# Four transposes of the identity behind every transpose of a gathered block, in the first stage of a recommender kernel

## The chip, the cores and the metric

The kernel runs on one core of a Trainium2 chip. The metric is the time of one execution on the device, in microseconds (us); smaller is better. Times of a kernel are medians of several runs. Engines are named as in the profile: PE is TensorE's matmul, PEld its weight load, DVE is VectorE, ACT is ScalarE, POOL is GpSimd and SP is SyncE. L335 is line 335 of the kernel before.

## What is computed

There are B = 1024 users with T = 50 items each, and a table of N = 100001 item embeddings of D = 128 numbers. For each user the running mean of the gathered embeddings is taken, normalised over the users, and sent through a spiking neuron; the spikes are averaged over time, and the averages are multiplied with the whole table.

```python
emb = emb_table.at[0].set(0.0)
e = emb[seq]                                   # 1024 x 50 x 128
prefix = jnp.cumsum(e, axis=1)
denom = jnp.minimum(t_idx[None, :], lengths[:, None]).astype(e.dtype)
uF = prefix / denom[:, :, None]
mean, var = uF.mean(axis=0), uF.var(axis=0)
y = (uF - mean) * lax.rsqrt(var + BN_EPS) * gamma + beta

def step(v, x):
    v = v + (x - v) / TAU
    spike = atan_spike(v - V_TH)
    return (v - spike * V_TH, spike)
_, spikes = lax.scan(step, v0, jnp.moveaxis(y, 1, 0))
scores = spikes.mean(axis=0) @ emb.T           # 1024 x 100001
```

## The kernel before

The kernel has two stages. The order of the work on every engine is written out by hand (`manual_schedule`): each engine runs its instructions in program order, and waits only where one needs what another engine has made.

**First stage: 50 steps, one for each position t.** Embeddings lie transposed on the chip, D on the 128 partitions and the 1024 users along the free axis, in two halves h of 512.

- `gather(t)` (L207) issues eight indirect DMAs from POOL, each fetching 128 rows of the table into a block of the tile `e`. There are two tiles `e`, used in turn; gather(t + 2) is issued in step t and overwrites the tile that step t reads, so it waits until TensorE has read it.
- For each of the eight blocks TensorE transposes the block by a matmul with the identity (L324) and adds it to the running sum `pre[h]` in PSUM. Half 0 has the first four blocks, half 1 the last four.
- After each half DVE makes the running mean `uF` from `pre[h]` (L335) and its statistics (L336).
- `correct(t + 1)` (L282) then adds to each half of `pre` a matmul that cancels row 0 of the table. It overwrites what L335 has read, so each of the two waits for the L335 of its half, and the next step's transposes come after both.
- DVE and ACT turn the statistics into scale and shift and update the membrane `v`, the reset and the count of spikes (L298, L301, L353, L376, L379, L294). This is one chain from step to step.
- In steps 42 and 44 the first two blocks of the table are prepared for the second stage: eight plain transposes each (L136) and a split into two parts by ACT (L152) and DVE (L153).

`keep_busy(tile, times)` (L308 to L310) issues transposes of a tile into `warm`, a PSUM tile of two banks that nothing reads and that becomes the tile `po0` of the second stage afterwards. In the kernel before it is called in the last step only: four transposes of the identity behind each of the first three blocks of half 1 (L333, L334), and sixteen of `near` after the loop (L415).

**Second stage.** The counts (1024 x 128) are multiplied with the table, block by block: transposes of a table block (L136), a split into two parts, products into PSUM (L160), a scaled copy by DVE or ACT (L512, L514), and stores of the 410 MB of scores by SP. Its first products wait for the count of the first 128 users (`countA`, L367), the end of the first stage's chain.

Of the kernel before, what the change touches and what calls it, by code (L numbers as in the profile page):

```python
# [20 lines left out]
P = 128  # L21
# [4 lines left out]
BANK = 512  # L26
# [13 lines left out]
def rec_kernel(  # L40
# [131 lines left out]
    with ExitStack() as ph:  # L172
# [135 lines left out]
        def keep_busy(tile, times):  # L308
            for k in range(times):
                nc.tensor.transpose(warm[:, k % KQ * P : (k % KQ + 1) * P], tile, ident)  # L310
# [6 lines left out]
        for t in range(T):  # L317
            last = t == T - 1
# [3 lines left out]
            for h, cs in enumerate(halves):  # L322
                for k in range(0, BANK, P):
                    nc.tensor.matmul(  # L324
                        pre[h][:, k : k + P],
                        lhsT=e[:, h * BANK + k : h * BANK + k + P],
                        rhs=ident,
                        start=False,
                        stop=last,
                        is_transpose=True,  # L330
                        skip_group_check=True,
                    )
                    if last and h and k + P < BANK:  # L333
                        keep_busy(ident, KQ // 2)  # L334
                nc.vector.scalar_tensor_tensor(uF[:, cs], rlen[:, cs], 1.0 / (t + 1), pre[h], ALU.max, ALU.mult)  # L335
                nc.vector.bn_stats(bs[:, h, :], uF[:, cs])  # L336
# [127 lines left out]
    for c, W in enumerate(WIDTHS):  # L464
# [34 lines left out]
        for n in range(NB):  # L499
# [26 lines left out]
            if n in (1, 4) and c >= MIDDLE and to_fetch < parts:  # L526
                g, k = divmod(to_fetch - SHIFT, GROUP)
# [26 lines left out]
```

## Time and profile before

| | us |
|---|---|
| median of 3 runs | 1633.66 |
| lowest, highest | 1633.3, 1634.7 |
| the profiled execution's own time | 1638.64 |
| its span, first to last instruction | 1636.8 |
| first gather starts, last gather ends | 3.4, 565.1 |
| PE busy in the span | 1085.8 (66%) |
| DVE busy | 948.7 (58%) |
| ACT busy | 673.0 (41%) |
| POOL busy | 381.1 (23%) |

How to read the profile. The page gives busy times, then the span in 40 equal slices of 41 us (each digit a tenth; PEclk is the TensorE clock granted, DMA the mean busy share of the 16 DMA engines), then the costliest groups of instructions. A group's line has the source line, the engine, the operation, output<-inputs, shapes and xcount, then its busy time and mean duration in ns, then the idle time of the engine just before these instructions and what ended most of it. A line of the list of waits has the waiting engine and line, what it waited for, the sum in us, how many times, and the longest. A line of the timeline has start and duration in us, then the instruction, and in brackets the idle time of its engine before it. "remote" and "issue" there mean that the profile found no instruction that ended the wait.

### The profile page before, as it was taken

The page shows a single profiled execution, that of the slowest core. Times are in us where ns is not written, and L with a number is a line of the kernel's source. Part 1 is how long each engine was busy: PE and PEld are TensorE (multiplying, and loading weights), DVE is VectorE, ACT ScalarE, POOL GpSimd, SP SyncE. Part 2 cuts the span into 40 slices and gives each one's busy share as a digit, 9 for nine tenths or more (in the row PEclk, how much of TensorE's full clock was granted, in tenths as well). Part 3 has the DMA queues.
Part 4 walks back from the last instruction along what each step waited for, and adds up shares of the span by engine and source line. Part 5 has one row for each costly group of instructions (what it writes and reads, how often), then busy time and mean ns, then how long its engine had stood idle before and what let it go on. Part 6 is the DMA issues. An engine that isn't in the chain of part 4 may idle for free.

```text
span 1636.8 us, 12254 instructions
## 1 busy us (share of the span) xinstructions
PE 1085.8 (66%) x4464; PEld 806.9 (49%) x4464; DVE 948.7 (58%) x1127; ACT 673.0 (41%) x697; POOL 381.1 (23%) x406
## 2 busy tenths in 40 slices
PE   4333332333332488888988877888878888788884
PEld 2212111222112366666766666666666666566663
DVE  5666654677665865665755554555545555555652
ACT  2333322333323354555554444444444444444442
POOL 7666666766666500000000000000000000000000
PEclk7555555555555599999999999989999999999998
DMA  9611111111111279999999999999999999999998
GB/s 346 240 46 46 46 45 46 51 45 47 45 46 47 66 326 412 415 423 412 405 426 430 427 428 429 403 432 426 418 428 420 408 423 426 427 424 408 429 401 358
DMA packets 51313, 488.12 MB, mean 298 GB/s; under 512 B 10079, under 2 KB 10336, under 8 KB 30004
## 3 DMA queue, kind: packets, MB, share of 16 engines
q1 hardware_dynamic: 30752, 430.86, 62.6%
q0 software_dynamic: 12800, 26.24, 5.4%
q10 hardware_dynamic: 7700, 30.23, 4.5%
q8 instruction: 35, 0.57, 0.1%
q14 instruction: 26, 0.21, 0.0%
HBM read 77.69 MB, written 409.60 MB: 298 GB/s over the span
## 4 chain that ended last, share of the span: by engine, by line
DMA 42%; PE 16%; DVE 14%; another core or an unknown queue 9%; POOL 7%; issue 5%; ACT 5%; ACTq 0%; SPq 0%; DVEq 0%; POOLq 0%
DMA scores<-o 40%; PE po L160 14%; POOL e L207 7%; DVE o L512 3%; ACT o L514 3%; DVE uF L335 2%; DVE bs L336 2%; DMA e<-in_L_rec_emb_table,idx 2%; DVE v L379 2%; DVE negv L298 1%; ACT v L376 1%; PE pre L324 1%; DVE count L301 1%; DVE pairs L153 1%
## 5 line engine op out<-in xcount | busy, mean ns | idle before, releaser
L512 DVE TENSOR_SCALAR o<-po 128x1024 f32<-128x1024 f32 (+1 forms) x391 | 467.4, 1214 | 326.0 <-DMA scores<-o 183.8
L514 ACT ACTIVATE o<-po 128x1024 f32<-128x1024 f32 x391 | 391.8, 1025 | 503.9 <-DMA scores<-o 358.6
L207 POOL DMA_INDIRECT e<-in_L_rec_emb_table,idx x400 | 380.4, 951 | 183.5 <-issue 110.9
L160 PE MATMUL po<-pairs,countB 128*128 128x512 f32 (+1 forms) x1120 | 291.2, 406 | 61.1 <-ACT o L514 61.1
L160 PE MATMUL po<-pairs,countC 128*128 128x512 f32 (+1 forms) x840 | 237.8, 430 | 59.0 <-ACT o L514 53.1
L160 PEld LDWEIGHTS po<-pairs,countB 128*128 128x128 f32 x1120 | 210.4, 193 | 122.0 <-ACT o L514 80.0
L282 PE MATMUL pre<-zT,ls 128*128 128x512 f32 x100 | 78.4, 786 | 271.2 <-DVE uF L335 227.2
L160 PEld LDWEIGHTS po<-pairs,countC 128*128 128x128 f32 x840 | 166.2, 205 | 111.0 <-ACT o L514 65.0
L282 PEld LDWEIGHTS pre<-zT,ls 128*128 128x128 f32 x100 | 29.0, 291 | 309.9 <-DVE uF L335 255.7
L324 PE MATMUL pre<-ident,e 128*128 128x128 f32 x400 | 126.8, 435 | 79.5 <-DMA e<-in_L_rec_emb_table,idx 63.0
L335 DVE SCALAR_TENSOR_TENSOR uF<-rlen,pre 128x512 f32<-128x512 f32 x100 | 68.0, 680 | 161.7 <-remote 124.4
L324 PEld LDWEIGHTS pre<-ident,e 128*128 128x128 f32 x400 | 80.4, 209 | 126.8 <-DMA e<-in_L_rec_emb_table,idx 94.7
L153 DVE TENSOR_TENSOR pairs<-pt,pairs 128x1024 fp32r<-128x1024 f32 x70 | 85.3, 1218 | 96.1 <-ACT pairs L152 96.0
L346 ACT ACTIVATE r<-mv,eps 128x1 f32<-128x1 f32 x50 | 14.8, 295 | 273.0 <-DVE mv L342 181.0
L136 PE MATMUL pt<-ident,rows 128*128 128x128 f32 (+1 forms) x768 | 105.6, 283 | 9.9 <-issue 4.9
L136 PEld LDWEIGHTS pt<-ident,rows 128*128 128x128 f32 (+1 forms) x768 | 95.1, 148 | 27.4 <-issue 11.5
L160 PE MATMUL po<-hi,countB 128*128 128x512 f32 x208 | 85.4, 411 | 13.9 <-ACT o L514 13.6
L152 ACT CAST pairs<-pt 128x1024 fp32r<-128x1024 f32 x70 | 70.1, 1013 | 41.0 <-PE pt L136 41.0
L160 PE MATMUL po<-lo,countB 128*128 128x512 f32 x208 | 83.2, 400 | 0.0
L294 ACT ACTIVATE d<-v,less 128x1024 bf16<-128x1024 f32 x49 | 54.5, 1113 | 65.4 <-DVE v L379 36.3
L160 PE MATMUL po<-hi,countC 128*128 128x512 f32 x156 | 66.5, 426 | 14.2 <-ACT o L514 12.6
L376 ACT ACTIVATE v<-uF,hgb,a 128x1024 f32<-128x1024 f32 x49 | 59.2, 1208 | 31.0 <-DVE a L372 11.7
(88 smaller groups left out, 887.2 us busy)
## 6 DMA issues: line engine op xcount, KB each, us to landing
scores<-o SPq DMA_DIRECT2D x96, 3072.0 KB
scores<-o SPq DMA_DIRECT2D x32, 1536.0 KB
scores<-o SPq DMA_DIRECT2D x30, 1024.0 KB
rows<-in_L_rec_emb_table ACTq DMA_DIRECT2D x19, 1536.0 KB
scores<-o SPq DMA_DIRECT2D x8, 2896.5 KB
rows<-in_L_rec_emb_table SPq DMA_DIRECT2D x5, 3072.0 KB
e<-in_L_rec_emb_table,idx POOLq DMA_INDIRECT x400
rows<-in_L_rec_emb_table SPq DMA_DIRECT2D x2, 1024.0 KB
```

The source lines that it names most:

```text
L136: nc.tensor.transpose(pt[:, k0 : k0 + pw], r[:pw, k0 : k0 + D], ident[:pw, :pw])
L152: nc.scalar.copy(vh, vp)
L153: nc.vector.tensor_tensor(vl, vp, vh.bitcast(F32), ALU.subtract)
L160: nc.tensor.matmul(po[:, :kw], lhsT=counts[n], rhs=part[:, k0 : k0 + kw], start=j == 0, stop=j == 1,)
L207: nc.gpsimd.indirect_dma_start(out=es[t][:, n * P : (n + 1) * P], out_offset=None, in_=table, in_offset=bass.IndirectOffsetOnAxis(ap=idx[: ...
L282: nc.tensor.matmul(pre[h], lhsT=l, rhs=zT[:, h * BANK : (h + 1) * BANK], start=t == 0, stop=False, skip_group_check=True,)
L294: nc.scalar.activation(d, v, AF.Identity, bias=less)
L324: nc.tensor.matmul(pre[h][:, k : k + P], lhsT=e[:, h * BANK + k : h * BANK + k + P], rhs=ident, start=False, stop=last, is_transpose=True, ...
L335: nc.vector.scalar_tensor_tensor(uF[:, cs], rlen[:, cs], 1.0 / (t + 1), pre[h], ALU.max, ALU.mult)
L376: nc.scalar.activation(vt, uF[:, cs], AF.Identity, bias=hgb[:, 1:2], scale=a)
L512: nc.vector.tensor_scalar_mul(o[:, h0 : h0 + hw], po[:, :hw], 1.0 / T)
L514: nc.scalar.mul(o[:, h0 : h0 + hw], po[:, :hw], 1.0 / T)
```

## The change

One condition is changed. In steps 0 to 48, `keep_busy(ident, 4)` is now called behind every one of the eight transposes of gathered blocks, in both halves. In the last step it is called where it was. Four transposes write the four quarters of the first bank of `warm`.

```diff
@@ -330,7 +330,7 @@
                         is_transpose=True,
                         skip_group_check=True,
                     )
-                    if last and h and k + P < BANK:
+                    if not last or h and k + P < BANK:
                         keep_busy(ident, KQ // 2)
                 nc.vector.scalar_tensor_tensor(uF[:, cs], rlen[:, cs], 1.0 / (t + 1), pre[h], ALU.max, ALU.mult)
                 nc.vector.bn_stats(bs[:, h, :], uF[:, cs])
```

The function that it calls, unchanged:

```python
def keep_busy(tile, times):
    for k in range(times):
        nc.tensor.transpose(warm[:, k % KQ * P : (k % KQ + 1) * P], tile, ident)
```

## The prediction

> **What bounds the kernel now.** I read the page's slices first, then its groups.
>
> ```profile
> PEclk7555555555555599999999999989999999999998
> DMA  9611111111111279999999999999999999999998
> ...
> L207 POOL DMA_INDIRECT e<-in_L_rec_emb_table,idx x400 | 380.4, 951 | 183.5 <-issue 110.9
> ...
> L324 PE MATMUL pre<-ident,e 128*128 128x128 f32 x400 | 126.8, 435 | 79.5 <-DMA e<-in_L_rec_emb_table,idx 63.0
> ```
>
> The slices show two stages. From slice 15 on the DMA engines are full (9 tenths, 416 GB/s from 579.5 us to the end in the table by stretches). Before that, for about 565 us, TensorE's clock is at half and the DMA engines are nearly idle: the first stage, the only one the diff changes. Its one engine without rest is POOL: 400 gathers, one every 1.248 us (0.944 busy, 0.304 of issue), 499 us in all, the first at 3.4 us and the last ending at 565.1. The missing 63 us are in the list of waits:
>
> ```profile
> POOL e L207 <- issue: 110.9, 364, 0.3
> POOL e L207 <- remote: 50.0, 10, 5.8
> POOL e L207 <- PE pre L282: 13.7, 3, 5.4
> ```
>
> POOL stood still 13 times, 63.7 us together. The timeline shows one such stop:
>
> ```profile
> 216.15 0.47 PE L324 MATMUL pre<-ident,e 128*128 128x128 f32 x1 [0.76 <-DMA e<-in_L_rec_emb_table,idx]
> ...
> 223.63 0.95 POOL L207 DMA_INDIRECT e<-in_L_rec_emb_table,idx  x1 [0.30 <-issue]
> ...
> 229.84 0.69 DVE L335 SCALAR_TENSOR_TENSOR uF<-rlen,pre 128x512 f32<-128x512 f32 x1 [4.91 <-remote]
> 230.07 0.94 POOL L207 DMA_INDIRECT e<-in_L_rec_emb_table,idx  x1 [5.50 <-remote]
> ```
>
> The last transpose of a step starts at 216.15, yet VectorE (L335) and POOL, which wait for TensorE's semaphore alone, go on at 229.8 and 230.1. TensorE's completions arrive late. The trace's semaphore records put them on a grid of 0.70 us in such a stretch (226.28, 228.38, 229.78), the rest within 0.1 us; elsewhere they follow the matmul's end within 0.05 us. TensorE looks guilty, and filling its idle time would look like a cure. I read it otherwise, from POOL's restarts after its stops: 59.60 (40 gathers since 3.40), 94.34 (24), 139.81, 184.95, 230.07 (32 each), 286.62 (40, with a short stop inside), 331.83, 377.04, 422.27, 467.43, 512.84 (32 each), 535.48 (16). Divided by the gathers between them: 1.405, 1.448, 1.421, 1.411, 1.410, 1.414, 1.413, 1.413, 1.413, 1.411, 1.419, 1.415 us. Whether 16, 24, 32 or 40 gathers lie between, a gather costs 1.41 us, twice 0.70. So something behind the gathers serves them at 1.41 us; POOL issues at 1.248, gets ahead, and the excess is paid back in a stop. 400 x 1.41 = 564 us is the stage. Late completions are how the queue makes itself felt, not what makes it long.
>
> The trace holds a test. In one such stretch the kernel puts eight more transposes (L136) on TensorE:
>
> ```profile
> 496.34 1.94 PE L136 MATMUL pt<-ident,rows 128*128 128x128 f32 x8 [4.87 <-issue]
> ...
> 512.33 1.01 ACT L152 CAST hi<-pt 128x1024 fp32r<-128x1024 f32 x1 [15.11 <-remote]
> 512.84 0.94 POOL L207 DMA_INDIRECT e<-in_L_rec_emb_table,idx  x1 [5.76 <-remote]
> ```
>
> Their completion comes 14 us late too, but the period around them (467.43 to 512.84) is 45.4 us for 32 gathers, like its neighbours. Extra matmuls neither shortened nor lengthened the stage.
>
> **What the Trainium skill says.** "TensorE: Matmul & The Clock Gate", Part 4 (PE-mode transpose), holds that transposes do not raise TensorE's clock. This trace disagrees: after some 17 transposes back to back (564.3 to 568.1) the clock is 1.00 in 569 to 571. "Perfetto Trace Analysis", Tensor Engine Instruction, says that a matmul's reported end is an estimate; the 216.15 line, signalled at 229.8, agrees. "Advanced Engine Details and Errata", Engine Queue Depths, gives TensorE a queue of 64; the trace shows at least 21 matmuls with their weight loads (42 instructions) started between 563.75 and 568.2 while the first was not signalled until 568.6.
>
> **The change part by part.** It removes nothing and moves nothing. Of 50 steps, 49 get 8 x 4 = 32 more transposes with as many weight loads: 1568 pairs, 3136 instructions.
>
> *TensorE's time.* Eight transposes back to back read 1.91 us, of which the last's tail is 0.42: 0.213 us each at half clock (0.107 at full, from the 568 us region). Five per gather take 1.06 us, under the 1.248 between gathers. A step: 40 x 0.213 = 8.5, plus two corrections (L282, 0.79 busy, the second waiting for L335), 1.5: 10.0 us at half clock, about 6 at full. The gathers give 8 x 1.41 = 11.3 us. Hidden, barely at half clock: cost 0. Without that cover it would be a few us a step.
>
> *Who queues behind the dummies.* The correction of the next step sits behind four (0.85 us), but it waits for L335 anyway (0.68 us after the last transpose): 0.2 us a step, off the path, since DVE needs 7.35 us of 11.3. The next transpose waits for its gather anyway. The bank po0 has no other user until the end. TensorE's 12 extra instruction fetches of 16 KB meet DMA engines at 0.15 to 0.2: 0.
>
> *Late stretches.* There each pair now crawls: by the semaphore records a matmul takes four 0.70 us slots while gathers run (266.61, 269.40, 272.20) and two when they stand (464.33, 465.75, 467.14). A step's 42 pairs cannot be signalled in a stretch; they come at its end at once, if they have been executed. In the 22 us of a stretch some 20 instructions pass; with 42 to 64 outstanding that is 62 to 84 of a step's 84. So at the end 0 to 22 instructions (11 pairs, 2.3 us) remain before POOL can go on, while its server idles. 12 stretches: 0 to 28 us; I take 1 us each, **12 us**.
>
> *Passing through.* If a pair took server time: the eight at 496 changed the period by less than 0.3 us, so under 0.03 us a pair; 14 pairs passed in 0.15 us at 569.4, 0.01 a pair, 17 us for all. Lower bound 0 (they slip in beside gathers): I take 0.
>
> *The end of the stage.* Here lateness is on the path:
>
> ```profile
> 563.00 0.69 DVE L335 SCALAR_TENSOR_TENSOR uF<-rlen,pre 128x512 f32<-128x512 f32 x1 [5.54 <-issue]
> ...
> 565.40 1.06 PE L310 MATMUL warm<-ident 128*128 128x128 f32 x4
> ...
> 570.90 0.68 DVE L335 SCALAR_TENSOR_TENSOR uF<-rlen,pre 128x512 f32<-128x512 f32 x1
> ```
>
> Step 48's second half is signalled at 563.0, in a late stretch that ends at 569.3; its DVE chain of 7.9 us ends at 570.9 and everything after follows. With four dummies in each gap that signal is held to the stretch's end, 569.5: **+6.5 us**. Range 0 (no stretch at the end) to 14 (step 47 held too). A warmer clock afterwards saves nothing, as products wait for countA. POOL's 1.41 us admits no gain unless dummies change it.
>
> Sum against the profiled execution, 1638.6 (span 1636.8 and 1.8 around it): 1638.6 + 12 + 6.5 = 1657. It lies 5 us over the median 1633.7; from the median, **1652**.
>
> **Rivals.**
> *Cure.* Lateness comes from an idle TensorE, and dense transposes end it. For: it arises only in the half-clocked stage, and the clock does rise. Against: 1.41 us a gather at every period, and the eight at 496. It gives back POOL's stops: 1633.7 - 63.7 = **1570**, faster; it decides if POOL falls to 1.248.
> *No effect.* All is absorbed: the step executes ahead within each stretch and the last stretch ends early. For: 10.0 us fits in 11.3. Against: the 563.0 signal. **1634**.
> *TensorE's completions become the bound.* If signals go late after some 45 queued instructions instead of after some 20 us, each step falls into a stretch: 10 us of gathers, 5 us until the queue empties, 2 of rest, 17 against 11.3: 49 x 5.7 = 280, **1913**. Against: the burst at 496 did no such thing. That the change doesn't do what it says can't be: each dummy is an instruction.
>
> **How the numbers follow.** Forecast 0.60, no effect 0.21, cure 0.12, completions as bound 0.07. The forecast's own range takes 0 to 28, 0 to 17 and 0 to 14: 1634 to 1693. Leaving out cure and bound (0.19), the range is 1631 to 1700. This kernel's measurement can tell about 0.2% (3.3 us) from no change. Slower by more: 0.60 + 0.07 = 0.67; faster 0.13 with a little luck at the end; the same 0.20.
>
> **What would show it.** Right: POOL's restarts still at 1.41 us a gather; L310 with 1596 matmuls (28 before); long L335 waits kept or longer; stops of 5 to 8 us; the last L335 pair 5 to 10 us later; nothing changed after 580 us. Clock: 1.0 in part of the stage. Wrong: POOL at 1.248 without stops (cure), or stops every 8 gathers (bound).

## The result, and the profile after

The changed kernel takes 1654.53 us (median of 4 runs, 1652.91 to 1656.01) against 1634.18 us (4 runs, 1633.3 to 1635.9) of the kernel before: ratio 1.0116 [1.0104, 1.0128], 20 us slower. The forecast was 1652. In the profiled executions the span went from 1636.8 to 1654.2 us. (The two profiled executions, 1638.64 and 1656.01 us, lie 4.5 and 1.5 us over these medians, so the traces show 17.4 of the 20 us; the rest can't be placed.) All of their difference lies in the first stage: the first product (L160) starts at 592.92 instead of 575.75, 17.17 us later, and from there to the end it is 1061.3 us instead of 1061.0.

The page of the changed kernel, slices first, then groups (busy us, mean ns, idle before and what ended it):

```profile
PEclk9877777787778789999999999989999899998998
DMA  9611111111111259999999999999999999999998
...
L207 POOL DMA_INDIRECT e<-in_L_rec_emb_table,idx x400 | 380.8, 952 | 196.4 <-issue 106.9
L310 PE MATMUL warm<-ident 128*128 128x128 f32 x1580 | 292.2, 320 | 59.1 <-issue 58.8
...
L335 DVE SCALAR_TENSOR_TENSOR uF<-rlen,pre 128x512 f32<-128x512 f32 x100 | 68.1, 681 | 184.5 <-remote 152.5
...
L324 PE MATMUL pre<-ident,e 128*128 128x128 f32 x400 | 128.3, 322 | 14.7 <-issue 14.7
```

The clock of the first stage reads 7 to 8 tenths where it read 5, and a transpose of a gathered block 322 ns where it took 435. The stage is longer all the same: POOL's gathers cost it nothing more (952 ns against 951), but its idle time rose from 183.5 to 196.4. Neither the faster clock nor the shorter transposes were on the path. The list of waits shows what was:

```profile
DVE uF L335 <- remote: 152.5, 40, 8.7
...
POOL e L207 <- issue: 106.9, 350, 0.6
POOL e L207 <- remote: 64.8, 31, 3.5
...
POOL e L207 <- PE pre L324: 18.7, 6, 4.3
```

The line on L335 in the kernel before:

```profile
DVE uF L335 <- remote: 124.4, 18, 10.0
```

Before, VectorE at L335 waited 18 times for a signal of TensorE that came late, up to 10.0 us; now it is 40 times, up to 8.7. POOL stood still 10 + 3 times for 63.7 us, in stops of up to 5.8 us; now 31 + 6 times for 83.5 us, in shorter ones. More and shorter stops: two of them in the timeline of the changed kernel (start, duration, instruction, idle time before it).

```profile
483.06 0.94 POOL L207 DMA_INDIRECT e<-in_L_rec_emb_table,idx  x1 [0.30 <-issue]
486.76 0.69 DVE L335 SCALAR_TENSOR_TENSOR uF<-rlen,pre 128x512 f32<-128x512 f32 x1 [8.70 <-remote]
487.22 0.94 POOL L207 DMA_INDIRECT e<-in_L_rec_emb_table,idx  x1 [3.22 <-remote]
...
495.96 0.94 POOL L207 DMA_INDIRECT e<-in_L_rec_emb_table,idx  x1 [0.31 <-issue]
498.57 0.94 POOL L207 DMA_INDIRECT e<-in_L_rec_emb_table,idx  x1 [1.67 <-remote]
```

VectorE and POOL restart within half a microsecond of each other, as at 229.8 and 230.1 in the kernel before: both were held by TensorE's signals. But eight gathers lie between the two restarts, sixteen before the first of them, where it was mostly 32. From first to last gather it is now 1.437 us per gather (3.57 to 578.48) instead of 1.404. The end of the stage:

```profile
580.17 0.69 DVE L335 SCALAR_TENSOR_TENSOR uF<-rlen,pre 128x512 f32<-128x512 f32 x1 [2.99 <-remote]
...
588.07 0.68 DVE L335 SCALAR_TENSOR_TENSOR uF<-rlen,pre 128x512 f32<-128x512 f32 x1
589.39 0.67 DVE L335 SCALAR_TENSOR_TENSOR uF<-rlen,pre 128x512 f32<-128x512 f32 x1
...
592.92 0.76 PE L160 MATMUL po<-hi,countA 128*128 128x512 f32 x1 [1.04 <-DVE a L368]
```

The same first product in the kernel before:

```profile
575.75 0.48 PE L160 MATMUL po<-hi,countA 128*128 128x512 f32 x1 [1.24 <-DVE a L368]
```

Step 48's second half (580.17) used to be signalled 2 us before the last gather ended (563.00 against 565.1); now it is signalled 1.7 us after it (578.48). The chain of 7.9 us behind it has not changed.

**An account of the queue.** To split the 17.17 us I count the gathers as customers of something that serves them one at a time in 1.400 us (the figure is that of the first experiment below). A gather that POOL issues while the queue is empty ends an idle piece; the idle pieces are what the stage loses against 400 x 1.400 = 560 us.

| traced execution | stops over 1 us | idle, us | queue empty at | first product | between |
|---|---|---|---|---|---|
| before | 14 | 5.7 | 569.1 | 575.75 | 6.6 |
| changed | 32 | 16.4 | 580.0 | 592.92 | 12.9 |
| difference | 18 | 10.7 | 10.9 | 17.17 | 6.3 |

In both executions one of the stops is the first gather's wait for the indices (2.1 and 2.3 us), and has nothing to do with TensorE. The account can be tried on the signals, which it doesn't use. The last L335 that a late signal holds starts at 580.17 us here, and at 580.15, 571.80, 581.58, 583.97 and 586.17 in the runs e3, e4, e5, e9b and e11 below, where the account has the queue empty at 580.0, and at 579.8, 571.7, 581.4, 583.8 and 585.9. By this account 10.9 us come from the pace and 6.3 from the end. The prediction had 12 and 6.5.

### The profile page after: what moved, and what is told of

It is laid out like the page before. It is cut to its first block, busy times and chain, and to the rows that moved or that the text cites. A ratio compares the mean times of both kernels' runs of the same rounds, so it can differ in the third digit from the quotient of the medians.

```text
span 1654.2 us, 15390 instructions
## 1 busy us (share of the span) xinstructions
PE 1251.1 (76%) x6032; PEld 1013.5 (61%) x6032; DVE 950.8 (57%) x1127; ACT 673.1 (41%) x697; POOL 381.5 (23%) x406
## 4 chain that ended last, share of the span: by engine, by line
DMA 41%; DVE 22%; PE 17%; another core or an unknown queue 10%; ACT 6%; issue 3%; ACTq 0%; SPq 0%; DVEq 0%
DMA scores<-o 41%; PE po L160 13%; DVE bs L336 4%; DVE uF L335 4%; DVE v L379 3%; DVE o L512 3%; DVE negv L298 3%; ACT o L514 3%; ACT v L376 2%; PE warm L310 2%; DVE count L301 1%; PE pre L324 1%; DVE a L372 1%; DVE pairs L153 1%
## 5 line engine op out<-in xcount | busy, mean ns | idle before, releaser
L512 DVE TENSOR_SCALAR o<-po 128x1024 f32<-128x1024 f32 (+1 forms) x391 | 467.8, 1214 | 325.6 <-DMA scores<-o 177.7
L207 POOL DMA_INDIRECT e<-in_L_rec_emb_table,idx x400 | 380.8, 952 | 196.4 <-issue 106.9
L310 PE MATMUL warm<-ident 128*128 128x128 f32 x1580 | 292.2, 320 | 59.1 <-issue 58.8
L160 PE MATMUL po<-pairs,countB 128*128 128x512 f32 (+1 forms) x1120 | 291.7, 407 | 58.6 <-ACT o L514 58.6
L310 PEld LDWEIGHTS warm<-ident 128*128 128x128 f32 x1580 | 238.0, 170 | 76.9 <-issue 75.3
L160 PE MATMUL po<-pairs,countC 128*128 128x512 f32 (+1 forms) x840 | 241.6, 436 | 56.6 <-ACT o L514 48.7
L160 PEld LDWEIGHTS po<-pairs,countB 128*128 128x128 f32 x1120 | 211.3, 194 | 119.0 <-ACT o L514 76.6
L160 PEld LDWEIGHTS po<-pairs,countC 128*128 128x128 f32 x840 | 169.4, 209 | 109.1 <-ACT o L514 60.8
L335 DVE SCALAR_TENSOR_TENSOR uF<-rlen,pre 128x512 f32<-128x512 f32 x100 | 68.1, 681 | 184.5 <-remote 152.5
L282 PE MATMUL pre<-zT,ls 128*128 128x512 f32 x100 | 61.9, 621 | 133.6 <-DVE uF L335 118.1
L282 PEld LDWEIGHTS pre<-zT,ls 128*128 128x128 f32 x100 | 22.8, 229 | 160.7 <-DVE uF L335 143.1
L160 PE MATMUL po<-hi,countB 128*128 128x512 f32 x208 | 85.5, 411 | 14.1 <-ACT o L514 13.7
L160 PE MATMUL po<-lo,countB 128*128 128x512 f32 x208 | 83.2, 400 | 0.0
L160 PE MATMUL po<-hi,countC 128*128 128x512 f32 x156 | 67.2, 431 | 13.3 <-ACT o L514 12.1
```

Source lines behind the costliest of these rows:

```text
L160: nc.tensor.matmul(po[:, :kw], lhsT=counts[n], rhs=part[:, k0 : k0 + kw], start=j == 0, stop=j == 1,)
L207: nc.gpsimd.indirect_dma_start(out=es[t][:, n * P : (n + 1) * P], out_offset=None, in_=table, in_offset=bass.IndirectOffsetOnAxis(ap=idx[: ...
L282: nc.tensor.matmul(pre[h], lhsT=l, rhs=zT[:, h * BANK : (h + 1) * BANK], start=t == 0, stop=False, skip_group_check=True,)
L512: nc.vector.tensor_scalar_mul(o[:, h0 : h0 + hw], po[:, :hw], 1.0 / T)
```

## The experiments

The theory on trial: something behind the gathers serves them at 1.40 us, a pile forms since POOL issues at 1.248, TensorE's signals are held up while there is a pile, and dummies cost time because more of TensorE's instructions wait in it. The rivals: POOL is slowed by TensorE's late signals alone and would run at 1.248 without them; or the dummies cost TensorE time of their own. The kernel before was timed on the chip of each group of runs, and its time is given with each. A pile is never seen directly in the profile; it is inferred from POOL's pace and the late signals. "A gather is served" is short for that: what is served is something that a gather leaves behind, and not the gather's data (see what is open).

**e1: POOL made free of TensorE.** The transposes read the identity instead of the gathered block, so that POOL waits for nobody.

```diff
-                        lhsT=e[:, h * BANK + k : h * BANK + k + P],
+                        lhsT=ident,
```

> The kernel before, with TensorE transposing the identity in place of the gathered blocks (the running sums are wrong), so that no gather waits for TensorE and TensorE waits for no gather; the last gathers still hold the second stage's first output buffers. Theory A (something behind the gathers serves them at 1.41 us each, whatever TensorE does): POOL's 400 gathers still take 555 to 570 us, and the whole some 1630. Theory B (TensorE's late completions are what stops POOL): POOL runs at 1.248 us without stops, its gathers end near 503 us and the whole is some 1572.

Measured: 1843.99 us, ratio 1.1235 [1.1202, 1.1268] against 1640.72. No forecast of the total foresaw that. The trace tells three things. POOL runs without stops at 1.256 us per gather up to about the 193rd (247 us), and then on its own at 1.4001 us, from the 195th to the 395th, though it waits for nobody. Second, VectorE's L335, half 0 of three steps (other lines between left out):

```profile
402.57 0.69 DVE L335 SCALAR_TENSOR_TENSOR uF<-rlen,pre 128x512 f32<-128x512 f32 x1 [11.36 <-remote]
...
430.57 0.69 DVE L335 SCALAR_TENSOR_TENSOR uF<-rlen,pre 128x512 f32<-128x512 f32 x1 [11.37 <-remote]
...
458.57 0.69 DVE L335 SCALAR_TENSOR_TENSOR uF<-rlen,pre 128x512 f32<-128x512 f32 x1 [11.37 <-remote]
```

A step takes 28.00 us, again and again. TensorE has 20 instructions in a step (ten matmuls, ten weight loads): 20 x 1.400. While the pile stands, TensorE's signals advance by one instruction per gather. Its work is not slowed; earlier in the same trace:

```profile
302.39 1.91 PE L324 MATMUL pre<-ident 128*128 128x128 f32 x8
...
318.55 0.69 DVE L335 SCALAR_TENSOR_TENSOR uF<-rlen,pre 128x512 f32<-128x512 f32 x1 [11.36 <-remote]
```

All eight transposes of the step are done at 304.3 us, and VectorE, which needs the first four, goes on at 318.55. Third, the account says that the pile is gone at 563.8 us; the steps take 28.0 us up to 525, and mostly 7.35 us from 565.6 on. So the queue is real, its rate does not come from TensorE's stops, and without those stops the pile never drains and TensorE pays. The rival with POOL at 1.248 fails from the 194th gather on; the prediction's theory missed the size, since it took the stops for a mere payback and not for what lets TensorE through.

**e2 and e2b: no gathers, without and with dummies.** From step 2 on the tile `e` is used again in place of a new gather.

```diff
-                gather(t + 2)
+                es[t + 2] = e
```

> The kernel before with gathers in the first two steps only; the later steps transpose the same blocks again (the result is wrong). Theory A: TensorE's completions are late only because of gathers, so no late stretches are left; the stage is DVE's 7.35 us a step, 370 us, and the whole some 1445. Theory B (an idle, half-clocked TensorE is late by itself): L335 still waits 5 to 10 us every few steps, and the stage is 420 us or longer.

> As e2_no_gathers, with the four dummies behind every transpose. Theory A: without gathers there are no late stretches, and the dummies cost TensorE's own time only: 10.0 us a step at half clock, about 6 at full; a busy TensorE gets full clock, so DVE's 7.35 to 8 us a step stay the bound and the whole is within 30 us of e2. Rival C (the dummies cost by their mere execution, gathers or not): the time over e2 is about as large as the 20 us seen with gathers, or larger.

Measured: 1466.37 us, ratio 0.8934 [0.8908, 0.8961], and with dummies 1471.45, both against 1640.72. The whole is longer than the 1445 forecast, with 7.7 us a step in place of 7.35, but the late signals are gone; in e2's list of waits L335 has one line left:

```profile
DVE uF L335 <- PE pre L324: 5.8, 2, 3.6
```

The dummies cost 5.1 us by the medians (7.2 in the traces, first product 402.54 and 409.75). This bounds what TensorE's own time for them costs in a stage with less to hide it (7.7 us a step where the gathers gave 11.3): 5 to 7 of the 20 us at most. Late signals need gathers.

**e3: dummies in steps 0 to 39 only.**

```diff
-                    if last and h and k + P < BANK:
+                    if t < 40 or last and h and k + P < BANK:
```

> The changed kernel with the dummies in steps 0 to 39 only. Theory A: the slower pace of the gathers (13.3 us over 49 steps in the traces) falls to 40/49, 11 us, and the 3.8 us at the end of the stage go: 1645. Rival D (the end of the stage carries most of the cost): 1637 to 1640. Rival E (the cost lies in the pace alone): 1650.

Measured: 1650.62 us, ratio 1.0067 [1.0045, 1.0089], 9.9 us over 1640.72 as medians and 11 by the ratio: the pace term alone. The forecasts were made against 1634; over the kernel before they are 11 us for theory A, 3 to 6 for D and 16 for E, so it is A that fits, though E's figure is the one met. The end of its trace:

```profile
580.15 0.69 DVE L335 SCALAR_TENSOR_TENSOR uF<-rlen,pre 128x512 f32<-128x512 f32 x1 [0.50 <-remote]
581.49 0.67 DVE L335 SCALAR_TENSOR_TENSOR uF<-rlen,pre 128x512 f32<-128x512 f32 x1
...
585.02 0.47 PE L160 MATMUL po<-hi,countA 128*128 128x512 f32 x1 [1.97 <-DVE a L368]
```

Queue idle 16.3 us, empty at 579.8, as in the changed kernel; the first product follows 5.2 us later and not 12.9. Without dummies near the end the second term is gone, and the first is there in full.

**e4 and e5: how many, or how long.** e5 keeps four dummies with a narrow weight load each (32 columns); e4 puts two wide matmuls (512 columns) in their place.

```diff
-                    if last and h and k + P < BANK:
+                    if not last:
+                        for j in range(KQ // 2):
+                            nc.tensor.transpose(warm[:32, j * P : (j + 1) * P], ident[:, :32], ident)
+                    elif h and k + P < BANK:
```

```diff
-                    if last and h and k + P < BANK:
+                    if not last:
+                        for _ in range(2):
+                            nc.tensor.matmul(warm[:, :BANK], lhsT=r0hi, rhs=zT[:, :BANK], start=True, stop=True)
+                    elif h and k + P < BANK:
```

> The changed kernel with each dummy's weight load cut to 32 of 128 columns: as many instructions, less of TensorE's time. Theory A2 (signals go late after a count of TensorE's instructions, whatever they are): as many stops of POOL (over 1 us) as with the change, 32 against 15 before, and the whole 17 to 21 us over before. Rival C (TensorE's time counts): fewer stops, 5 to 12 us over before.

> The changed kernel with two F32R matmuls of 512 columns in place of each four dummies: TensorE's time as large[...], half the added instructions. Theory A2 (count): stops between the two kernels (20 to 28), the gathers' pace between 1.404 and 1.437 us, and the whole 8 to 15 us over before. Rival C (time): as the change, 17 to 21 us over before.

Measured against 1635.63: e5 1656.0, ratio 1.0130 [1.0114, 1.0147]; e4 1641.9, ratio 1.0039 [1.0025, 1.0053], less than any of its forecasts. The waits of POOL, e5 first:

```profile
POOL e L207 <- remote: 66.7, 32, 3.5
POOL e L207 <- PE pre L324: 18.3, 6, 4.7
```

```profile
POOL e L207 <- remote: 63.3, 20, 4.3
POOL e L207 <- PE pre L324: 4.0, 1, 4.0
```

TensorE has 20 instructions in a step of the kernel before, 52 in e4, 84 in e5 and in the changed kernel; the stops over 1 us are 14, 22, 31 and 32. They grow with the count of instructions. That it is the count and not TensorE's time rests on e4: its dummies keep TensorE as busy as those of the change (286.1 us against 292.2), and half as many instructions bring half of the added stops (8 against 18). e5 can't tell the two apart: the narrower loads took 114 ns in place of 170, but the matmuls 319 in place of 320, one after another as before, so TensorE's time did not fall as expected. It shows only that the width of the load changes nothing. e4's cost does not halve but falls to a third of e5's. Its profiled execution (1647.5) is the slowest of its five, so its trace, with idle 8.2 us and 14.2 us from the empty queue to the first product, isn't that of its median; where the rest of e4's cost went stays open.

**e9 and e9b: POOL slowed to the queue's pace, without and with dummies.** If POOL issued at the pace at which gathers are served, no pile would form, and the dummies would cost nothing. A small memset on POOL behind each gather was to bring that about.

```diff
+        slow = once.tile([P, 16], F32, tag="slow", name="slow")
...
+                nc.gpsimd.memset(slow, 0.0)
```

> The kernel before with a small memset on POOL (128 x 16) behind every gather, to bring POOL's own pace from 1.248 us to 1.40 us or a little over; the extra time of a memset isn't known, 0.1 to 0.3 us. Theory A: when POOL no longer issues faster than 1.40 us, nothing piles up, TensorE is never late, POOL has no stops and the long waits of L335 on TensorE vanish; although POOL works more, the whole is 400 x (pace - 1.404) off before less 0 to 7 us at the end of the stage: the same or up to 5 us faster at a pace of 1.40, 18 us slower at 1.45. Theory B (POOL is stopped by TensorE's lateness alone): the stops stay as they are and the extra work adds its full 400 x (pace - 1.248), 60 us at 1.40.

> The changed kernel with the same memset behind every gather. Theory A: without a pile the dummies hide in TensorE's idle time, and cost at most 3 us over e9_paced in place of 20. Rival C (the dummies cost by their execution): about 20 us over e9_paced.

Measured against 1635.63: 1638.79, ratio 1.0033 [1.0022, 1.0044], and with dummies 1661.72, ratio 1.0161 [1.0144, 1.0178]. POOL in e9:

```profile
299.95 0.12 POOL L214 MEMSET slow<- 128x16 f32 x1
300.26 0.95 POOL L208 DMA_INDIRECT e<-in_L_rec_emb_table,idx  x1 [0.18 <-issue]
301.20 0.14 POOL L214 MEMSET slow<- 128x16 f32 x1
301.51 0.95 POOL L208 DMA_INDIRECT e<-in_L_rec_emb_table,idx  x1 [0.18 <-issue]
```

The memset fits into the 0.30 us between two gathers; they still start 1.25 us apart. The pacing failed, and the late signals stayed (L337 in e9, the same instruction as L335 before, waited 38 times for them, 143.3 us), and so did the dummies' cost: 22.9 us over e9 as medians. (e9's 18 runs lie in two groups, eleven of 1636.6 to 1639.4 us and seven of 1643.6 to 1645.5; all four of e9b lie above both.)

**e10 and e10b: two memsets, without and with dummies; e7: dummies in steps 40 to 48 only.** These three ran on one chip.

```diff
+        slow = once.tile([P, 64], F32, tag="slow", name="slow")
...
+                nc.gpsimd.memset(slow[:, :16], 0.0)
+                nc.gpsimd.memset(slow, 0.0)
```

```diff
-                    if last and h and k + P < BANK:
+                    if 40 <= t < T - 1 or last and h and k + P < BANK:
```

> As e9_paced with a second memset (128 x 64) behind every gather; in e9_paced the one memset vanished in the 0.30 us between gathers (1.255 us a gather), two should make 1.39 to 1.43. Theory A: at 1.40 us or over nothing piles up behind the gathers, POOL has at most a few stops, L335's long waits on TensorE shrink to those for a gather's landing, and the whole is 400 x (pace - 1.404) less up to 6 us off before: at 1.39 to 1.41 between 6 us faster and 3 slower, at 1.43 up to 10 slower. Theory B: the stops stay and 400 x (pace - 1.248) comes on top, 57 to 73 us.

> The changed kernel with the same two memsets. Theory A: without a pile the dummies hide in TensorE's idle time: at most 4 us over e10_paced2, in place of 20. Rival C (the dummies cost by their execution or their passing): 15 us or more over e10_paced2.

> The changed kernel with the dummies in steps 40 to 48 only. Theory A: the end of the stage brings 6.3 us (step 48's second half signalled when the queue behind the gathers is empty), the slower pace 9/49 of 11 us, 2: together 8 over before. Rival D (each step's dummies cost the same, the end nothing extra): 9/49 of 20, 4 us.

What no forecast had is the time of the kernel before on this chip: **1573.95 us** (23 runs, 1572.6 to 1575.24), 60 us under its time on the chips of the other groups. Against that, e10 took 1673.06, ratio 1.0629 [1.0611, 1.0647]; e10b 1670.96, ratio 1.0615 [1.0598, 1.0633]; e7 1571.66, ratio 0.9985 [0.9978, 0.9992]. The waits of e7, whose first 40 steps are those of the kernel before:

```profile
POOL e L207 <- issue: 118.3, 388, 0.3
DVE uF L335 <- PE pre L324: 108.4, 49, 3.6
...
POOL e L207 <- PE pre L324: 1.5, 5, 0.3
```

No stop of POOL for TensorE over 0.3 us, no wait of L335 that the profile can't put to a matmul, 1.252 us per gather from 3.46 to 504.45, and the first product at 510.1. On this chip nothing serves gathers at 1.40 us: 400 of them would have piled up 60 us by the account, and VectorE starts on the last one's sum (506.56) 3.1 us after POOL starts that gather (503.51). The 60 us are about what POOL's stops came to (63.7). With them goes what the experiments were to test. e10 slowed POOL for nothing (1.500 us per gather, +99 us = 400 x 0.248), and its comparison with the kernel before says nothing on the theory. What can be read is that dummies cost nothing here. e10b is 2.1 us under e10, with the first product 0.7 us later, though at 1.500 us per gather TensorE has more time than in the kernel before. e7, at 1.252, is the closer test, for nine steps: it is 2.3 us under the kernel before, where the end term of 6.3 us would have shown. A pace term of nine steps, 2 us, is too small to be told from that. L335 in e10, then in e10b:

```profile
DVE uF L338 <- PE pre L327: 203.8, 55, 5.7
```

```profile
DVE uF L338 <- PE pre L327: 205.4, 64, 5.8
```

The same waits, with 1568 more transposes. What e10b gains lies in the second stage (1061.9 us in e10, 1059.5 in e10b); no run here takes that apart, or says where e7 gains.

**e11: the changed kernel again, on another chip.**

> The changed kernel itself, once more, to see whether its cost hangs on the chip that runs it. The kernel before took 1634 to 1641 us on three chips and 1574 us on a fourth, and in the runs traced on that fourth (e7, e10, e10b) no gather piles up behind POOL's queue: POOL issues one in 1.25 us with one stop of 1.4 us in 400 gathers, and uF at L335 waits for its own product (3.6 us at most). Theory (the cost is made of the pile: it exists only where gathers are served at 1.40 us): if the kernel before takes about 1574 here, the changed one takes 1570 to 1576, ratio 0.997 to 1.001; if it takes 1634 to 1641, the changed one takes 18 to 22 us more, ratio 1.011 to 1.014. Rival 1 (the four transposes cost TensorE time of their own in the step, whatever the gathers do, as the 5 to 7 us without any gather suggest): 5 to 7 us more on a chip at 1574. Rival 2 (the transposes cause the late signals themselves): 15 us or more on either chip.

Measured: 1662.05 us (1660.88 to 1663.82), ratio 1.0127 [1.0098, 1.0156] against 1639.48. POOL's and L335's waits:

```profile
DVE uF L335 <- remote: 166.0, 37, 9.4
...
POOL e L207 <- remote: 73.0, 34, 3.5
...
POOL e L207 <- PE pre L324: 16.0, 5, 5.3
```

This chip has the queue, and the cost is there again, 22.6 us: idle 22.4 us, empty at 585.9, first product 14.3 us later. The changed kernel itself was not timed on the chip without the queue.

## Why the prediction was right, and where it was not

The direction, the size and both terms held: 10.9 us for 12, 6.3 us for 6.5. Two of its steps did not, and that the first term came out so close is luck. Its 1.41 us a gather is the 1.400 of e1 with the idle pieces (5.7 us in all) spread over it.

- **TensorE's time, hidden: right.** The 10.0 us at half clock were an upper end. In the changed kernel about half of the dummies follow each other in 0.109 us instead of 0.213, without gathers about two thirds, and the whole of them costs 5 to 7 us where the stage gives them less cover (e2b).
- **Late stretches: the sum right by luck, its making wrong.** The text kept the twelve stretches and took 1 us of leftovers at the end of each. The changed kernel has 18 more stops, and the queue idles 0.5 us in each (16.4 us in 32 stops). The failed premise is "In the 22 us of a stretch some 20 instructions pass; with 42 to 64 outstanding that is 62 to 84 of a step's 84": it lets a step finish within the stretch, so that POOL could go on. With 84 instructions in a step POOL has to stop after every 8 or 16 gathers, which e4 ties to the count of instructions. So 12 stretches of 1 us and 32 stops of 0.5 less 14 of 0.4 give nearly the same sum for different reasons.
- **Passing through, taken as 0:** the account needs no such term; no run tests it apart.
- **The end: right, and shown by e3.** Taking the dummies out of the last nine of their steps removes 7.7 us between the empty queue and the first product.
- **The test in the trace** (eight transposes at 496 us change nothing) was read too far. Eight more pairs are a quarter of what a step of the changed kernel adds, and come once.
- **Rivals.** *No effect* is excluded by the interval. *Completions become the bound* had the premise right (signals late by the count of instructions, stops after one or two steps) and the price wrong: it charged 5 us of draining to every step. By the account, draining takes what has piled up, 8 x 0.152 = 1.2 or 16 x 0.152 = 2.4 us, which is no loss. Only the rest of a stop is lost: of the median stops, 2.9 - 2.4 and 1.5 - 1.2. *Cure* has the right size for POOL's stops: without them the kernel takes 1574 us, and the rival said 1570. But they are missing there without any dummies, and on the other chips dummies made more of them.
- **The signs named beforehand:** long L335 waits were kept and multiplied (right); POOL's restarts at 1.41 us a gather became 1.44, and stops of 5 to 8 us became 1.3 to 4.0 (wrong, by the failed step); the last pair of L335 came 17.2 us later and not 5 to 10, since that sign left out the pace; part of the stage ran at full clock, and nothing changed after the first product (both right).

On the clock, the prediction doubted what the Trainium skill, "TensorE: Matmul & The Clock Gate", Part 4 (PE-mode transpose), holds, that transposes do not bring the full clock. The runs bear the doubt out. In the changed kernel 1212 of the 1214 transposes that follow the one before in 0.109 us fall where the trace records a clock of 1.00, and 589 of the 590 at 0.213 us with a record fall where it records 0.50. A page can mislead in this: e1's reads 9 tenths through its first stage, while eight transposes there took 1.91 us, 0.213 each and a tail. Its trace holds no record of the clock before 726 us. On the estimated end of a matmul, which the prediction saw in the line of 216.15: in e7 L335 starts 0.04 us after the reported end of the transpose that it waited for, all 50 times that VectorE stood waiting, so the 13.7 us of that line are the late signal and not the estimate.

**What is open.** What the queue is. It isn't the data: in the kernel before, in the changed kernel, in e1 and in e7, the first data packet of a gather starts 1.65 to 1.66 us after POOL begins to issue it (medians from the 80th gather on), with the queue as without. It isn't the gather's own signal either, as TensorE sees it. The transpose at 216.15 us, shown in the prediction, waited for this gather:

```profile
213.65 0.94 POOL L207 DMA_INDIRECT e<-in_L_rec_emb_table,idx  x1 [0.30 <-issue]
```

TensorE starts 2.5 us after POOL, though by the account 3.5 us of earlier gathers lie ahead of this one. In the kernel before there are 94 transposes that start within 2.6 us of their gather; in e7, without the queue, 2.6 us is the median. VectorE's signals are prompt as well: in e1's pile L335 ends at 403.26 us and L282, which waits for it, starts at 403.32. What the traces show late is TensorE's own signals.

It may be the recording of signals. The Trainium skill, "DMA: Bandwidth & Descriptors", Why a DMA increments its semaphore by 16 and not by 1, says that each of 16 DMA engines adds one to the semaphore of such a transfer. The traces agree: the packet lists of the kernel before, the changed kernel, e1, e3, e7 and e10 hold 16 packets of 4 bytes per gather, taken here for the increments, beside its 16 of data, and e7, e10 and e10b hold 15.97 to 16.00 records of the increments per gather. On the chips with the queue these records are 2.96 per gather in the kernel before, 1.75 in e1, 4.25 in the changed kernel. The packets are there and the records are not. Something that takes such records one by one, 16 of a gather and one of TensorE's in turn, would give one instruction of TensorE per gather. That is argued from the numbers and not shown, and it doesn't fit all of them: at a seventeenth of 1.40 us each, the 3136 instructions that the change adds would take 258 us, and the stage grew by 17. Whether the chip or the recording of these executions makes it slow no run here tells.

## What to carry to other kernels

Filling an idle engine helps only if its idleness or its clock is on the path: here TensorE got faster (322 ns for 435) and the kernel slower, on the chips with the queue, because its signals, and not its work, were what others waited for, and each added instruction is one more to wait behind. When waits end long after the instruction that they name, take away other work to see what the lateness needs (here the gathers, e2), and count instructions as well as their time (e4). And time the kernel before beside every variant on the same chip: between chips it moved by 60 us, three times what the change did.

## What the runs showed of the hardware that was not expected

- Indirect gathers of 128 rows of 512 bytes, issued one behind another by POOL: 1.248 us each on the issuing side, in stretches without stops. POOL is held to 1.400 us each in the end where nothing else stops it (e1), the end of TensorE's late signals fits the same figure in all four groups of runs that show them, and on the chip of a fifth there is no such limit (e7). TensorE can start on a block 2.5 us after its gather is issued in both cases. In e1 POOL was 193 gathers in before the limit reached it; by then it was some 20 gathers ahead (28 us by the account).
- While such a pile stands, TensorE executes at once and its signals advance one instruction per gather: 28.00 us for 20 (e1).
- A memset of 128x16 on POOL (0.12 to 0.14 us) fits between two gathers, which still start 1.25 us apart (e9); of two memsets, the second of 128x64, 0.25 us per gather remain (e10: 1.500 against 1.252).
